# Attention and Fourier layer on one core: softmax weights transposed in 32x32 blocks and moved by transfers, order of work computed

## Chip, cores, metric

The kernel runs on one core of a Trainium2 chip. The metric is the device time of one execution in microseconds (us); smaller is better. The engines are called as in the profile: PE (TensorE), DVE (VectorE), ACT (ScalarE), POOL (GpSimd) and SP (SyncE, which here only issues transfers).

## What is computed

Two layers over x, 4096 rows (2 batches of 2048) of 512 float32 numbers. The reference, cut:

```python
x = x + xattn(layernorm(x), ctx, mask)      # 16 heads of 32, 128 keys a batch
x = x + ffn(layernorm(x))
# xattn: q = n @ wq + bq; k, v from ctx
# score = q k^T / sqrt(32) * mask; score == 0 -> -1e9
# context = softmax(score) v;  return context @ wo + bo
# ffn: real(ifft(fft(n) @ (w_re + i w_im))) + bias
```

Everything is float32. The second layer is linear in n, so the kernel builds one 512x512 matrix `m_ffn` from the Fourier weights once and then multiplies by it.

## The kernel before

The rows are cut into 32 tiles of 128, taken in eight groups `i` of four tiles `t`. In a tile:

- `scores` (L316): 16 small matmuls (32 deep, 128x128) fill two PSUM tiles `sc`, one for each half of eight heads.
- `Softmax` for each half (L335): DVE multiplies by the mask (`masked`, L345); turns zeros into the masked value and the sign round (L352) and takes the maxima (L354, scaled in L355); ACT takes eight exponentials with their sums (`exponentials`, L361); `divided` takes the reciprocal of the sums on DVE (L373) and multiplies the 128x1024 weights by it on POOL (L374).
- `transposed_weights` (L380): PE transposes the 16 heads' 128x128 weights (L400), ACT copies them to `pt` (L391).

Once per group:

- `Queries` (L285): four chains `q` of four matmuls, 512 columns wide. `query_statistics`, `query_norm` and `query_transposes` prepare their input: `relative` takes each row less its first element, bn_stats and aggregation on DVE (L219, L220), the deviation on POOL (L223, L224), normalization on DVE (L227), four transposes on PE (L194), a copy on ACT (L196).
- `context` (L414): 16 matmuls (L426) of `v` with the transposed weights, four copies on ACT (L434) to `cT`.

And for each tile, one or two groups later: `Project` (L446) is a chain `o`, added to the residual on DVE (L463), where POOL has added the bias (L442); the second normalization by the same steps (`ffn_statistics`, `ffn_norm`, `ffn_transposes`, with POOL adding the other bias, L482); `Ffn` (L489) is a chain `y`, added on DVE (L528), and a store from SP (L529). Every chain's matmuls are L210, in `chain`.

A float32 matmul shows as two MATMUL records and a float32 transpose as one. PSUM has two `sc` tiles of two banks and two banks each in `ps_tp` and `ps_mm`.

The order is written out by hand: each engine runs its instructions in the order in which the code gives them, and waits on semaphores. `slot` (L770) lays out one tile: scores, masks, then up to three chains, with the weight transposes of the tile before (`turned`) between them; lists such as `early`, `pool`, `on_a` or `end` place the other pieces. The first six and the last three tiles are written out piece by piece. Transfers go through SP: `load_rows` (L120), `load_residual` (L127), `load_mask` (L132) and the stores.

The Fourier preparation (`First`, `Second`, L659 and L732, with `half` and `m` tiles) and the keys and values run once, between the first tiles.

## Time and profile before

| | us |
|---|---|
| median of three timed runs | 526.06 (525.54 to 526.25) |
| span of the profiled execution, first to last instruction | 525.0 |
| timed median less that span | 1.06 |
| PE busy in the span | 517.2 |
| DVE busy | 443.9 |
| ACT busy | 343.3 |
| POOL busy | 336.4 |
| DMA: mean rate over the span | 69 GB/s |

The span comes from one profiled execution, the times from others without a profile. Busy is the union of an engine's instructions; a matmul's end is modelled, so a busy PE may still have room, and the start of one piece to the start of the next is the safer measure. The granted clock of PE is full in every slice. In a row of the groups of instructions stand line, engine, operation, the tiles written and read, the shape and count; then busy us and mean ns of one; then the idle time ahead of it and who ended it.

### The profile page before, as it was taken

The numbers are of one execution on the slowest core, as the hardware profiler recorded it, in microseconds if no ns is written. First come the engines' busy times: TensorE is split into PE (matmuls) and PEld (weight loads), VectorE is DVE, ScalarE is ACT, GpSimd is POOL, SyncE is SP. The second block draws the span as 40 slices with busy tenths as digits, with TensorE's granted clock in tenths as the row PEclk, the third lists the DMA queues.
The fourth block names the chain that finished last, engine by engine and source line by source line (L and its number), as shares of the span: only waits on it lengthen the run. The fifth ranks groups of instructions, "written<-read, shape, count | busy, mean of one in ns | idle before, by whom it ended". The sixth has DMA issues, their size and how long they took to land.

```text
span 525.0 us, 8834 instructions
## 1 busy us (share of the span) xinstructions
PE 517.2 (99%) x3028; PEld 293.0 (56%) x3028; DVE 443.9 (85%) x616; ACT 343.3 (65%) x1298; POOL 336.4 (64%) x286
## 2 busy tenths in 40 slices
PE   8999999999899999999999999999999999999997
PEld 7856685655445554555545555455545555555444
DVE  4889899999987999889997999989986899998351
ACT  3367799876666677766667777666686667666210
POOL 2769569996982579634993559634664466766450
PEclk9999999999999999999999999999999999999999
DMA  8962020000600042000600024000312001301002
GB/s 318 387 238 80 1 83 21 0 2 19 223 2 21 1 159 82 1 21 1 220 22 21 1 87 156 0 22 0 121 42 80 21 19 44 101 1 61 20 0 81
DMA packets 22892, 36.49 MB, mean 69 GB/s; under 512 B 2104, under 2 KB 7488, under 8 KB 22848
## 3 DMA queue, kind: packets, MB, share of 16 engines
q1 hardware_dynamic: 22160, 34.75, 19.1%
q10 hardware_dynamic: 688, 1.18, 0.6%
q8 instruction: 24, 0.39, 0.3%
q14 instruction: 20, 0.16, 0.1%
HBM read 27.53 MB, written 8.39 MB: 68 GB/s over the span
## 4 chain that ended last, share of the span: by engine, by line
PE 72%; DVE 17%; ACT 4%; POOL 4%; issue 2%; DMA 1%; SPq 0%; ACTq 0%; POOLq 0%; DVEq 0%
PE y L210 17%; PE o L210 16%; PE q L210 14%; PE tpw L400 7%; PE sc L326 5%; DVE w L352 4%; PE c L426 4%; ACT w L361 4%; DVE nmax L354 4%; DVE w L345 3%; PE tp_f L194 2%; PE tp_a L194 2%; PE k L570 1%; POOL w L374 1%; DVE nmax L355 1%
## 5 line engine op out<-in xcount | busy, mean ns | idle before, releaser
L361 ACT ACTIVATE w<-w,nmax 128x128 f32<-128x128 f32 x512 | 198.3, 394 | 22.4 <-DVE nmax L355 18.4
L374 POOL TENSOR_TENSOR w<-w,rden 128x1024 f32<-128x1024 f32 x62 | 120.4, 1947 | 65.1 <-DVE rden L373 54.7
L210 PE MATMUL o<-wo,cT 128*128 128x512 f32 x256 | 115.4, 594 | 0.0
L210 PE MATMUL y<-m_ffn,nT 128*128 128x512 f32 x248 | 112.5, 595 | 0.3 <-DVE nT L198 0.2
L210 PE MATMUL q<-xnT,wq 128*128 128x512 f32 (+1 forms) x256 | 111.8, 581 | 0.4 <-ACT cT L434 0.2
L391 ACT COPY pt<-tpw 128x512 f32<-128x512 f32 x120 | 64.1, 587 | 56.0 <-PE tpw L400 55.8
L361 ACT ACTIVATION_READ_ACCUMULATOR w<-w,nmax 128x1 f32 x512 | 98.8, 193 | 0.0
L352 DVE SCALAR_TENSOR_TENSOR w<-w 128x1024 f32<-128x1024 f32 x64 | 96.8, 1513 | 0.9
L345 DVE TENSOR_TENSOR w<-sc,mask 128x1024 f32<-128x1024 f32 x64 | 77.4, 1211 | 8.7 <-PE sc L326 8.2
L354 DVE TENSOR_REDUCE nmax<-w 128x8 f32<-128x1024 f32 x64 | 78.1, 1220 | 2.2
L400 PEld LDWEIGHTS tpw<-ident,w 128*128 128x128 f32 x496 | 57.5, 141 | 30.9 <-issue 28.1
L210 PEld LDWEIGHTS o<-wo,cT 128*128 128x128 f32 x256 | 46.2, 190 | 47.8 <-issue 46.2
L210 PEld LDWEIGHTS q<-xnT,wq 128*128 128x128 f32 x256 | 46.4, 190 | 46.1 <-issue 40.2
L210 PEld LDWEIGHTS y<-m_ffn,nT 128*128 128x128 f32 x248 | 44.5, 190 | 45.3 <-issue 43.5
L400 PE MATMUL tpw<-ident,w 128*128 128x128 f32 x496 | 65.0, 273 | 0.5 <-POOL w L374 0.4
L482 POOL TENSOR_TENSOR x<-x,bf 128x512 f32<-128x512 f32 x32 | 45.5, 1422 | 29.7 <-DVE norm_f L227 29.7
L223 POOL TENSOR_SCALAR rstd_f<-mv_f 128x1 f32<-128x1 f32 x32 | 19.0, 595 | 57.4 <-DVE mv_f L220 57.4
L442 POOL TENSOR_TENSOR x<-x,bo 128x512 f32<-128x512 f32 x32 | 45.5, 1450 | 0.0
L244 POOL TENSOR_SCALAR rel<-rows 128x512 f32<-128x512 f32 x24 | 42.7, 1792 | 0.5 <-PE k L570 0.5
L326 PEld LDWEIGHTS sc<-kT,qT 32*128 32x128 f32 x1024 | 31.5, 186 | 13.6 <-issue 11.4
L196 ACT COPY nT<-tp_f 128x512 f32<-128x512 f32 x29 | 16.8, 581 | 33.5 <-PE tp_f L194 33.4
L326 PE MATMUL sc<-kT,qT 32*128 32x128 f32 x1024 | 37.5, 283 | 0.0
(96 smaller groups left out, 532.6 us busy)
## 6 DMA issues: line engine op xcount, KB each, us to landing
rows<-in_x_dram SPq DMA_DIRECT2D x32, 256.0 KB, 4.6
x<-in_x_dram SPq DMA_DIRECT2D x32, 256.0 KB, 4.3
out_dram<-x SPq DMA_DIRECT2D x31, 256.0 KB, 2.0
mask<-in_mask_Bx1xSxS_fk_dram SPq DMA_DIRECT2D x8, 256.0 KB, 4.3
wk<-in_L_xattn_wk_w_dram ACTq DMA_DIRECT2D x2, 512.0 KB, 7.1
wq<-in_L_xattn_wq_w_dram SPq DMA_DIRECT2D x1, 1024.0 KB, 6.7
wr<-n_L_ffn_w_freq_real_dram SPq DMA_DIRECT2D x2, 512.0 KB
wi<-n_L_ffn_w_freq_imag_dram SPq DMA_DIRECT2D x2, 512.0 KB, 7.9
```

What stands on the lines that cost most here:

```text
L210: nc.tensor.matmul(ps, lhs(c), rhs(c), start=(c == 0), stop=(c == NC - 1))
L244: eng.tensor_scalar(d, xt, xt[:, 0:1], None, ALU.subtract)
L326: nc.tensor.matmul(sc[r // 2][:, r % 2, g, :], qTs[i][rows, g, t * P : (t + 1) * P], kT[rows, g, b * K : (b + 1) * K], start=True, stop=True,)
L345: nc.vector.tensor_tensor(self.w, self.sc.rearrange("p r g k -> p (r g) k"), self.mrow, ALU.mult)
L352: nc.vector.scalar_tensor_tensor(w, w, 0.0, w, ALU.is_equal, ALU.subtract)
L354: nc.vector.tensor_reduce(self.nmax, w, AX.X, ALU.min)
L361: nc.scalar.activation(w[:, h, :], w[:, h, :], AF.Exp, bias=self.nmax[:, h : h + 1], scale=-UNIT, accum_out=self.den[:, h : h + 1],)
L374: eng.tensor_tensor(w, w, rden.unsqueeze(2).to_broadcast([P, HH, K]), ALU.mult)
L391: nc.scalar.copy(dst, ps)
L400: nc.tensor.transpose(ps[:, r, :], ws[r // 2].w[:, (r % 2) * NC + g, :], ident)
L442: nc.gpsimd.tensor_tensor(xs[:, t, :], xs[:, t, :], bo, ALU.add)
L482: nc.gpsimd.tensor_tensor(xt, xt, bf, ALU.add)
```

## The change

The weights are no longer divided, and are no longer transposed on PE, except in the last tile.

- `blocks`: DVE transposes each half in 32x32 blocks (one instruction of 128x1024), into `Tw`. A block stays in its 32 partitions.
- `exchange`: 16 transfers a tile from SP move the blocks between the four sets of 32 partitions, each 32 rows of 2 KB (64 KB), from `Tw` to `pt`. A `pt` tile now holds the weights of two tiles.
- `Context`: the sums `den` of a whole group are inverted and transposed on DVE (`inverse`), written to HBM by eight small transfers (`collect`) and read back by four broadcasting ones of 256 KB (`spread`) into `rb`; `evict` multiplies the context by `rb` on DVE on its way out of PSUM. `pe` uses 32 matmuls of 256 columns, read in runs of 32.
- `Norm`: bn_stats works on the rows themselves (`relative` is gone); POOL forms deviation and `shift`, and ACT normalizes.
- `ps_tp` is merged into `ps_mm` (four banks); `w` has four buffers instead of five, `xnT` two instead of one.
- The written-out order and `slot` are gone. Behind the first tile's preparation every piece is entered with engine, cost, rank, needs and the buffers that it takes and gives; `emit` goes through them while the program is built and always takes the piece that its own clock lets start first (within `PATIENCE`, the lowest rank). That clock is arithmetic in the kernel's Python; on the chip the engines still only follow the resulting order and the semaphores. It treats POOL's pieces and DVE's `zeros` as excluding each other (`locks`).

The core of the diff:

```diff
-        def divided(self, eng=nc.gpsimd):
-            w = self.w
-            rden = small.tile([P, HH], FP, tag="rden", name=f"rden_{self.n}")
-            nc.vector.reciprocal(rden, self.den)
-            eng.tensor_tensor(
-                w, w, rden.unsqueeze(2).to_broadcast([P, HH, K]), ALU.mult
-            )
...
-    def transposed_weights(i, t, first, end, eng=None, banks=None, later=None):
-        if t == 0 and first == 0:
-            pts[i] = [big_tile("pt", 6, f"pt_{i}_{g}") for g in range(NC)]
-        ws = weights[i, t]
-        def copy(g, ps):
-            dst = pts[i][g][:, :, t * P : (t + 1) * P]
-            if eng:
-                eng.tensor_copy(dst, ps)
-            else:
-                nc.scalar.copy(dst, ps)
-        for g in range(first, end):
-            ps = (
-                banks[g]
-                if banks
-                else ps_tp.tile([P, NR, P], FP, tag="tp", name=f"tpw_{i}_{t}_{g}")
-            )
-            for r in range(NR):
-                nc.tensor.transpose(
-                    ps[:, r, :], ws[r // 2].w[:, (r % 2) * NC + g, :], ident
-                )
-            if later is not None:
-                later.append((copy, g, ps))
-            elif not banks:
-                copy(g, ps)
-        if banks and later is None:
-            for g in range(first, end):
-                copy(g, banks[g])
...
-    def context(i, first, end, eng=nc.scalar, spare=False):
-        b = place(i)[0]
-        if first == 0:
-            cTs[i] = big_tile("cT", 1, f"cT_{i}")
-        cT = cTs[i]
-        for g in range(first, end):
-            pool, tag = (ps_tp, "tp") if spare and 0 < g < NC - 1 else (ps_mm, "mm")
-            ps = pool.tile([P, GQ], FP, tag=tag, name=f"c_{i}_{g}")
-            for r in range(NR):
-                h = g * NR + r
-                nc.tensor.matmul(
-                    ps[r * DH : (r + 1) * DH, :],
-                    v[:, b, h * DH : (h + 1) * DH],
-                    pts[i][g][:, r, :],
-                    start=True,
-                    stop=True,
-                )
-            if eng is nc.scalar:
-                nc.scalar.copy(cT[:, g, :], ps)
-            else:
-                eng.tensor_copy(cT[:, g, :], ps)
...
+        def shift(self):
+            s = self.less = small.tile([P, 1], FP, tag="less", bufs=6, name=f"less_{self.name}")
+            nc.gpsimd.tensor_scalar(s, self.mv[:, 0:1], self.rstd, -1.0, ALU.mult, ALU.mult)
+        def norm(self, eng=None):
+            self.n = row_tile(self.tag, self.bufs, f"{self.tag}_{self.name}")
+            if eng is None or eng is nc.scalar:
+                nc.scalar.activation(
+                    self.n, self.src(), AF.Identity, bias=self.less, scale=self.rstd
+                )
...
+        def blocks(self, hf):
+            if hf == 0:
+                self.T = big.tile([P, NR, H, DH], FP, tag="Tw", bufs=2, name=f"Tw_{self.n}")
+            nc.vector.transpose(
+                self.T[:, :, hf * HH : (hf + 1) * HH, :],
+                self.w[hf].rearrange("p h (b j) -> p b h j", b=NR),
+            )
+        def exchange(self, b):
+            dst = weights_of(self.n)
+            for a in range(NR):
+                nc.sync.dma_start(
+                    dst[b * DH : (b + 1) * DH, a, :, :],
+                    self.T[a * DH : (a + 1) * DH, b, :, :],
+                )
...
+        def turn(self, hf, k):
+            ps = self.ps[hf, k] = bank(f"tpw_{self.n}_{hf}_{k}")
+            for r in range(NC):
+                nc.tensor.transpose(ps[:, r, :], self.w[hf][:, k * NC + r, :], ident)
+        def turned(self, hf, k, eng):
+            h = hf * HH + k * NC
+            copy(
+                eng,
+                weights_of(self.n)[:, :, h : h + NC, :].rearrange("p a h i -> p h a i"),
+                self.ps.pop((hf, k)).rearrange("p h (a i) -> p h a i", a=NR),
+            )
...
+    class Context:
+        def __init__(self, i):
+            self.i, self.ps = i, {}
+        def inverse(self):
+            den = dens.pop(self.i).rearrange("p t h -> p (t h)")
+            nc.vector.reciprocal(den, den)
+            self.rdT = small.tile([P, 2, DH], FP, tag="rdT", bufs=1, name=f"rdT_{self.i}")
+            nc.vector.transpose(self.rdT.rearrange("p k i -> p (k i)"), den)
+        def collect(self):
+            self.rd = dram.tile([H, GQ], FP, tag="rd", name=f"rd_{self.i}")
+            to = self.rd.rearrange("h (k t a i) -> a t h k i", k=2, t=2, a=NR)
+            for a in range(NR):
+                for t in range(2):
+                    p0 = a * DH + t * H
+                    nc.sync.dma_start(to[a, t], self.rdT[p0 : p0 + H])
+        def spread(self):
+            self.rb = big_tile("rb", 1, f"rb_{self.i}")
+            src = self.rd.rearrange("(r g) n -> r g n", g=NC)
+            for r in range(NR):
+                nc.sync.dma_start(
+                    self.rb[r * DH : (r + 1) * DH], src[r].partition_broadcast(DH)
+                )
+        def pe(self, g):
+            i = self.i
+            b = where(i * TG)[0]
+            ps = self.ps[g] = bank(f"c_{i}_{g}").rearrange("p a n -> p (a n)")
+            for u in range(2):
+                for r in range(NR):
+                    h = g * NR + r
+                    nc.tensor.matmul(
+                        ps[r * DH : (r + 1) * DH, u * 2 * P : (u + 1) * 2 * P],
+                        v[:, b, h * DH : (h + 1) * DH],
+                        pts[i * 2 + u][:, :, :, r * NC + g, :],
+                        start=True,
+                        stop=True,
+                    )
+        def evict(self, g):
+            i = self.i
+            if g == 0:
+                cTs[i] = big_tile("cT", 1, f"cT_{i}")
+            nc.vector.tensor_tensor(
+                cTs[i][:, g, :], self.ps.pop(g), self.rb[:, g, :], ALU.mult
+            )
...
+    LINK = 0.1
+    ROOM = {
+        "mm": 4, "sc": 2, "w": WBUFS, "Tw": 2, "norm": 2, "nf": 2, "nT": 2, "pt": 3,
+        "cT": 1, "xnT": 2, "qT": 2, "rows": 4, "x": 2, "mask": 2, "lane": 8, "rb": 1,
+    }
+    PATIENCE = {"PE": 0.3, "DVE": 0.2, "ACT": 0.15, "POOL": 0.2, "SP": 0.0}
...
+            for entry in waiting:
+                rank, k, p = entry
+                begin = max([q.end for q in p.needs], default=0.0)
+                for t in set(p.takes):
+                    n = p.takes.count(t)
+                    begin = max(begin, sorted(room[t])[n - 1] if len(room[t]) >= n else 1e9)
+                if begin >= 1e9:
+                    continue
+                for e, cost in p.engines:
+                    start = max(begin, free[e])
+                    if p.locks and e in held:
+                        start = max(start, held["POOL" if e == "DVE" else "DVE"])
+                    if e == "PE" and p.mode != mode:
+                        start = max(start, free[e] + 0.2)
+                    options.setdefault(e, []).append((start, rank, k, entry, cost))
+            best = None
+            for e, os in options.items():
+                first = min(o[0] for o in os)
+                o = min((o for o in os if o[0] <= first + PATIENCE[e]), key=lambda o: o[1:3])
+                if best is None or o[:3] < best[0]:
+                    best = o[:3], e, o
...
+            if p.kb:
+                arrived = max(arrived, start + 0.6) + p.kb / 280.0
+                p.end = max(free[e], arrived) + 1.4
+            else:
+                p.end = free[e] + LINK
...
+    def load(count, kb, rank, f, needs=(), takes=(), gives=()):
+        return piece(
+            [("SP", 0.43 * count)], rank, f, needs, list(takes) + ["lane"] * count,
+            list(gives) + ["lane"] * count, kb=kb * count,
+        )
+    SLOT = 13.6
...
+        for hf in range(2):
+            t0 = n * SLOT + hf * 5
+            p = dve(1.12, t0 + 1.3, lambda s=s, hf=hf: s.masked(hf), [sc, mask_in[i]], ["w"], ["sc"])
+            p = dve(1.12, t0 + 2.5, lambda s=s, hf=hf: s.zeros(hf), [p], locks=True)
+            p = dve(1.13, t0 + 3.6, lambda s=s, hf=hf: s.maxima(hf), [p], gives=["mask"] if t == TG - 1 and hf else [])
+            p = dve(0.09, t0 + 4.8, lambda s=s, hf=hf: s.units(hf), [p])
+            e1 = act(1.55, t0 + 5, lambda s=s, hf=hf: s.exponentials(hf, 0), [p])
+            e2 = act(1.55, t0 + 6.5, lambda s=s, hf=hf: s.exponentials(hf, 1), [e1])
+            exps.setdefault(i, []).append(e2)
...
+            if not last:
+                p = b_ = dve(1.13, t0 + 10.2, lambda s=s, hf=hf: s.blocks(hf), [p, b_], ["Tw"] if hf == 0 else [], ["w"])
...
+        if not last:
+            for b in range(NR):
+                p = load(
+                    4, 64, n * SLOT + 17, lambda s=s, b=b: s.exchange(b), [p],
+                    ["pt"] if n % 2 == 0 and b == 0 else [], ["Tw"] if b == NR - 1 else [],
+                )
...
+            need = sum((moved[i * TG + k] for k in range(TG)), [values_done])
+            d = dve(0.25, t0 - SLOT, c.inverse, exps[i])
+            d = load(8, 2, t0 - SLOT + 1, c.collect, [d])
+            d = load(4, 256, t0 - SLOT + 4, c.spread, [d], ["rb"])
```

## Prediction

> **What bounds the kernel now.** I read the page's first two parts, then the groups of instructions, then TensorE's timeline for one tile, then the waits of each engine, and last SyncE's timeline.
>
> ```profile
> span 525.0 us, 8834 instructions
> PE 517.2 (99%) x3028; PEld 293.0 (56%) x3028; DVE 443.9 (85%) x616; ACT 343.3 (65%) x1298; POOL 336.4 (64%) x286
> ```
>
> TensorE has 7.8 us without work. A busy PE need not be a needed PE, so I checked with one tile's timeline (start, duration):
>
> ```profile
> 115.58 1.17 PE L326 MATMUL sc<-kT,qT 32*128 32x128 f32 x32
> 116.68 1.09 PE L194 MATMUL tp_a<-ident,rel 128*128 128x128 f32 x8
> 117.61 3.60 PE L210 MATMUL o<-wo,cT 128*128 128x512 f32 x8
> 121.04 1.04 PE L400 MATMUL tpw<-ident,w 128*128 128x128 f32 x8
> 121.92 3.60 PE L210 MATMUL y<-m_ffn,nT 128*128 128x512 f32 x8
> 125.35 1.04 PE L400 MATMUL tpw<-ident,w 128*128 128x128 f32 x8
> 126.23 3.60 PE L210 MATMUL q<-xnT,wq 128*128 128x512 f32 x8
> 129.66 0.60 PE L194 MATMUL tp_f<-ident,norm_f 128*128 128x128 f32 x4
> ```
>
> Read starts, not durations: each piece begins before the modelled end of the one in front. A chain holds PE 3.43 us, scores 1.10, eight transposes 0.87, nothing idles. A tile's true demand is three chains 10.3, scores 1.1, weight transposes 1.75, two row transposes 0.95, a quarter of a context (3.58) 0.9: 15.0. SyncE's row loads for successive groups start at 190.17, 250.46 and 310.75, which is 60.3 per four tiles, 15.07 each. So PE sets the pace in every tile, and what is taken from PE counts in full until something else is late.
>
> The next in line is VectorE:
>
> ```profile
> L352 DVE SCALAR_TENSOR_TENSOR w<-w 128x1024 f32<-128x1024 f32 x64 | 96.8, 1513 | 0.9
> L345 DVE TENSOR_TENSOR w<-sc,mask 128x1024 f32<-128x1024 f32 x64 | 77.4, 1211 | 8.7 <-PE sc L326 8.2
> L354 DVE TENSOR_REDUCE nmax<-w 128x8 f32<-128x1024 f32 x64 | 78.1, 1220 | 2.2
> L374 POOL TENSOR_TENSOR w<-w,rden 128x1024 f32<-128x1024 f32 x62 | 120.4, 1947 | 65.1 <-DVE rden L373 54.7
> ```
>
> L352's median is 1225 ns and its longest 3190: the excess, 64 x 0.29 = 18 us, comes where it overlaps POOL, as at 255.25, where it took 2.49 beside L374 and L244.
>
> **The change, on TensorE.** It removes 16 transposes from each of 31 tiles (the last keeps them): 31 x 1.75 = 54 us. The context takes twice as many matmuls of half the columns, with its moving operand in runs of 32 elements. Bounds: nothing, to 128 further pairs of weight loads at 0.109 (28 us), if none lay behind matmuls. I take nothing: scores issue 32 loads in 1.10 us, and the strided loads of L677 took 196 ns against 190. PE alone would thus end at 525.0 - 54 = **471**.
>
> **On VectorE.** Removed: both normalizations (L227, 64 instructions, 59 us, to ACT), 64 reciprocals (0.11 from start to start), odd copies. Added: 62 block transposes, 32 context evictions with the inverse sums (0.64 each, as L463 and L528), eight small reciprocals and transposes. No row shows a VectorE transpose. Below, it costs 0.9 (two L227 of 512 elements, 0.45 apart when free); above, 2.44 (L354 twice). I take 1.17, L354's length less the 0.05 by which instructions overlap on average: it also reads one f32 input of 1024 elements.
>
> A page of the Trainium skill, "VectorE: DVE Perf Modes", section "Rules for kernel authors", speaks against the change: a 128x128 transpose belongs on TensorE. Its table "The three transpose paths" gives VectorE 311 ns for one 128x128 square; eight by themselves would be an estimated 2.49 us per half, 62 x 1.3 = 82 us above my sum, so about 575. I weigh it as one long instruction. No run here shows it yet.
>
> Per tile, from start to start (when free): mask 1.17, zeros 1.2, maxima 1.2, units 0.09, block transpose 1.17, all twice: 9.7. Three evictions at 0.64: 1.9. Two bn_stats with aggregation at 0.82: 1.6. Together **13.2**, against PE's 15.0 - 1.75 = 13.3. Contention stays where POOL reads beside `zeros`. POOL loses L374 and L244 (163 us) and keeps both bias additions (2 x 45.5) and two deviations a tile. Today's excess is 18 us on L352 and 10 on L355 (0.327 against 0.17). Bounds 0 and 28; I take 5, since the new order keeps `zeros` and POOL work apart, though only by its own clock.
>
> **The sum.** VectorE's first mask stays at 21.3. 32 x 13.2 = 422.4; contention 5; preparation after 21.3 (values 1.2; eight pairs L711 and L712, four at 1.48, four at 0.81) 10.4; less the last tile's block transposes, 2.4; less what VectorE does after the last softmax (context 2.6, projection and statistics 5.8, output 2.6, some two outputs still behind, 1.3) 12.3. The last maximum ends at 21.3 + 422.4 + 5 + 10.4 - 2.4 - 12.3 = 444.4.
>
> Then a chain that is now serial: eight exponentials 3.1, inverse 0.3, eight `collect` issues at 0.46 and one landing 2.0 (rows_m, the only SBUF to SBUF transfer in the trace), four `spread` issues 1.8 and a landing 4.3 (that of x), eviction 0.6: 15.8. Outputs of the group before run on PE meanwhile. From the first o of the last group to the end took 492.26 to 525.0, 32.7 now. 444.4 + 15.8 + 32.7 = **492.9**. Timed runs have a median of 526.06, 1.06 above this span: 494.
>
> **What I cost at nothing, and its cover.** ACT loses 31 x 4 copies at 0.5, gains two normalizations of 0.6 a tile; 16 exponentials 6.2 plus five other passes is 9 of 13.3. POOL has about 6 of 13.3. Uncovered, a copy delays a chain by its 0.6. A longer normalization (POOL's shift, 0.25) lies beside earlier outputs; without these, 0.25 each in the last group. SyncE gets 16 exchange transfers a tile, 2 collect, 1 spread, ahead of the loads and stores that wait in its order: 22.25 issues with row, residual, store and mask. Its pace:
>
> ```profile
> 190.17 1.82 SPq L120 DMA_DIRECT2D rows<-in_x_dram  x4
> 192.04 0.42 SPq L132 DMA_DIRECT2D mask<-in_mask_Bx1xSxS_fk_dram  x1
> 192.56 1.90 SPq L127 DMA_DIRECT2D x<-in_x_dram  x4
> 200.66 49.70 SPq L529 DMA_DIRECT2D out_dram<-x  x4
> ```
>
> Four issues in 1.82 to 1.90: 0.46 each, 10.2 a tile. The 49.70 is waiting for outputs: there is room. About 2.1 MB a tile in 13.4 us is 157 GB/s; the first 20 us moved 347. An exchange waits for the second block transpose, and loads and stores queue behind it. Rows are ranked nine tiles ahead of their use; a late store holds one residual buffer.
>
> Another page, "DMA: Bandwidth & Descriptors", sections "Bandwidth" and "Rules for kernel authors", advises against many small transfers and gives 0.95 us for 64 KB. Sixteen end to end would be an estimated 15.2 us a tile, above the pace, and the end, by the third rival's formula below, about 549 instead of 493. The x loads, issued 0.46 apart and landing after 4.3, already overlap here.
>
> **The rivals.**
>
> *TensorE stays the bound.* If a block transpose is 0.9 (62 x -0.27 = -17) and contention nil (-5), VectorE's path ends at 471, level with PE's 471, and 1 to 10 us of bubbles bring 472 to 482. For: L227 when free. Against: it has no reshaping to do. I give 0.20.
>
> *VectorE costs more.* At L374's 1.35 on VectorE, the transposes add 62 x 0.18 = 11; contention at half of its old 28 adds 9; an exchange landing at 4.3 instead of 2.0 adds some 2 for each of 8 contexts if PE has no other work, 16. Singly or together: 503 to 524, typically 510. For: the order is fixed by costs in the kernel that leave out POOL's lock on `units`. Against: neighbours of a stalled piece remain ready. 0.15.
>
> *SyncE's queue becomes the pace, and the kernel is slower.* In the loading stage four rows took 2.93 (start 8.88), 0.73 an issue. The last tile's scores are then at 21.3 + 31 p, its maximum some 8 later, its end 48.5 after that. This passes 525 when p is above 14.4, that is 0.65 an issue. At 0.73, p = 16.2: 580; at 0.67, p = 14.9: 540. For: 16 of these issues must run in order behind a wait. Against: at a quarter to a half of the DMA engines' load the rows show 0.46. That the exchange adds more work than it hides is this case too. 0.14.
>
> The forecast itself, VectorE and TensorE nearly level with VectorE late, covers 482 to 503 and has 0.50. Within 0.2% of the present time, about what a measurement can tell from no change, I leave 0.01, between the rivals. **So** faster 0.85, same 0.01, slower 0.14. The range 472 to 518 takes in the forecast, nearly all of the first rival and two thirds of the second.
>
> **What will show it.** The L400 group falls from 512 to 16; VectorE's busy share rises above 92% and PE's falls to 95% or so; row loads come about 54 us per group. The block transpose's mean: 1.2 supports the sum, above 1.7 it would be slower by that alone (32 us in 62). SyncE issue spacing tells the third rival. PE's waits by name show whether context waits for exchange landings. A granted clock below 1.0, through PE gaps, would void every PE price here.

## The result and the profile after

The changed kernel takes **577.07 us** (median of four runs, 575.61 to 577.9) beside 525.92 for the kernel before on the same chip: 1.097 times as long (95% interval 1.095 to 1.099). The forecast was 494, faster. The profiled execution has a span of 576.1 us, 83 more than the 492.9 of the sum. The head of the page, with TensorE's busy row and the granted clock by slices:

```profile
span 576.1 us, 8985 instructions
...
PE 492.4 (85%) x2788; PEld 259.6 (45%) x2788; DVE 446.3 (77%) x592; ACT 307.3 (53%) x1202; POOL 186.3 (32%) x298
...
PE   8869988557997999869997999899989984996797
...
PEclk9979998967999899989997999999999997899799
```

No engine is full any more. PE lost 25 us of busy time, not 54, because its pieces also stretched: where its row falls to 4, 5 or 6, the clock of that slice or the next falls to 6 to 8 tenths. Now three groups of instructions: two on VectorE, the new one and the one that contended with POOL, and the context on PE (busy us, mean ns, then idle time in front and who ended it):

```profile
L356 DVE STREAM_TRANSPOSE Tw<-w 128x1024 f32<-128x1024 f32 x62 | 76.2, 1233 | 32.9 <-DMA pt<-Tw 25.8
...
L327 DVE SCALAR_TENSOR_TENSOR w<-w 128x1024 f32<-128x1024 f32 x64 | 82.1, 1283 | 0.7
...
L421 PE MATMUL c<-pt,v 128*32 128x256 f32 x512 | 43.7, 500 | 35.4 <-DMA pt<-Tw 33.6
```

The disputed prices of VectorE came out as taken: a block transpose lasts 1.23 (1.17 was taken from start to start, the first began at 47.94 and the next instruction at 49.11), and `zeros` has a mean of 1283 instead of 1513, so contention, against the median of 1225 before, is 64 x 0.06 = 4 us. What is new stands at the end of the first and the last line: the block transposes wait 25.8 us for exchange transfers to free `Tw`, and PE waits 33.6 us in front of the contexts for exchanges to land. The contexts also stretched most: 43.7 us, against 29.4 (L426) in the kernel before. The chain that ended last, shares by engine, before; then the same and the shares by line, after:

```profile
PE 72%; DVE 17%; ACT 4%; POOL 4%; issue 2%; DMA 1%; SPq 0%; ACTq 0%; POOLq 0%; DVEq 0%
```

```profile
SPq 27%; PE 26%; DVE 20%; DMA 16%; ACT 4%; issue 4%; POOL 1%; DVEq 0%; ACTq 0%
SPq L365 19%; PE y L188 6%; PE o L188 6%; DMA rb<-rd 5%; SPq L403 5%; PE q L188 5%; DMA pt<-Tw 4%; DVE Tw L356 4%; DVE w L327 3%; DVE w L318 3%; DMA rd<-rdT 3%; DVE nmax L331 2%; ACT w L343 2%; PE c L421 2%; DMA x<-in_x_dram 2%
```

Before, SyncE's queue (SPq) held 0% of the chain. Now it is first, most of it `exchange`'s line L365. This is SyncE's timeline around the first group's context, and under it two of PE's pieces of the same time, with the wait in front of each in brackets:

```profile
97.52 16.80 SPq L365 DMA_DIRECT2D pt<-Tw  x24
114.42 0.53 SPq L111 DMA_DIRECT2D rows<-in_x_dram  x1
114.99 2.40 SPq L365 DMA_DIRECT2D pt<-Tw  x4
117.50 0.53 SPq L111 DMA_DIRECT2D rows<-in_x_dram  x1
118.07 5.60 SPq L403 DMA_DIRECT2D rd<-rdT  x8
124.93 1.73 SPq L410 DMA_DIRECT2D rb<-rd  x4
126.78 2.44 SPq L365 DMA_DIRECT2D pt<-Tw  x4
129.32 0.52 SPq L111 DMA_DIRECT2D rows<-in_x_dram  x1
129.89 19.91 SPq L365 DMA_DIRECT2D pt<-Tw  x28
```

```profile
119.17 5.63 PE L421 MATMUL c<-pt,v 128*32 128x256 f32 x56 [10.41 <-DMA pt<-Tw]
...
133.48 5.80 PE L188 MATMUL q<-xnT,wq 128*128 128x512 f32 x8 [6.96 <-DVE cT L433]
```

Read the queue from top to bottom: from 97.5 to 150 it issues with hardly a gap, and `collect`, whose eight transfers carry 4 KB each, stands behind 28 exchanges. PE waits 10.4 us at the context for the last exchange, then 7.0 because that context holds all four banks until `spread` has landed. Behind these waits eight matmuls of q last 5.80 instead of the 3.60 of other places, at the lowered clock. The four exchanges at 114.99 hold the queue until the next piece starts at 117.50, and eight collects take 5.0 in other groups: **0.63 us** an issue for both forms. `spread` takes 0.43, loads and stores about 0.5. A tile thus takes 16 x 0.63 + 2 x 0.63 + 0.43 + 0.53 (row) + 0.5 (residual) + 0.53 (store) + 0.14 (mask) = 13.5 us of issuing (the expectations below reckon with 14 to 14.1). Is the queue really full? From the last maximum of the fourth tile to the very last one, 422.7 us, all of SyncE's waits add up to 44 us. The longest:

```profile
SPq L410 <- DMA rd<-rdT: 9.5, 11, 2.2
SPq L365 <- DMA x<-in_x_dram: 8.7, 11, 1.3
SPq L365 <- DMA rb<-rd: 6.0, 11, 0.9
```

The other 379 us are issuing, with the short steps from one issue to the next: 54.1 for each of seven groups, which is 4 x 13.5. SyncE is full there for 90% of the time.

**Three marks** make runs comparable: the start of the last maximum (`tensor_reduce`) of the fourth tile, the mean time from one group's last maximum to the next, and the time from the very last maximum to the end. In the forecast a group is 4 x 13.2 + 5/8 of contention = 53.4, the last maximum starts at 443.2 (444.4 is its end), so the fourth tile's at 443.2 - 7 x 53.4 = 69.4.

| | span | tile 4's last maximum | a group | last maximum | from there to the end |
|---|---|---|---|---|---|
| before | 525.0 | 72.1 | 58.3 | 480.4 | 44.6 |
| forecast | 492.9 | 69.4 | 53.4 | 443.2 | 49.7 |
| after | 576.1 | 90.8 | 60.4 | 513.5 | 62.6 |

The 83 us split into 21 at the start, 7 x 7.0 = 49 in the groups, and 13 at the end.

### The profile page after: what moved, and what is told of

The parts are those of the page before. It is cut to its first block, busy times and chain, and to the rows that moved or that the text cites. A ratio compares the mean times of both kernels' runs of the same rounds, so it can differ in the third digit from the quotient of the medians.

```text
span 576.1 us, 8985 instructions
## 1 busy us (share of the span) xinstructions
PE 492.4 (85%) x2788; PEld 259.6 (45%) x2788; DVE 446.3 (77%) x592; ACT 307.3 (53%) x1202; POOL 186.3 (32%) x298
## 4 chain that ended last, share of the span: by engine, by line
SPq 27%; PE 26%; DVE 20%; DMA 16%; ACT 4%; issue 4%; POOL 1%; DVEq 0%; ACTq 0%
SPq L365 19%; PE y L188 6%; PE o L188 6%; DMA rb<-rd 5%; SPq L403 5%; PE q L188 5%; DMA pt<-Tw 4%; DVE Tw L356 4%; DVE w L327 3%; DVE w L318 3%; DMA rd<-rdT 3%; DVE nmax L331 2%; ACT w L343 2%; PE c L421 2%; DMA x<-in_x_dram 2%
## 5 line engine op out<-in xcount | busy, mean ns | idle before, releaser
L188 PE MATMUL q<-xnT,wq 128*128 128x512 f32 (+2 forms) x288 | 119.3, 560 | 10.1 <-DVE cT L433 7.0
L188 PE MATMUL y<-m_ffn,nT 128*128 128x512 f32 x248 | 116.2, 613 | 0.7 <-ACT nT L195 0.7
L356 DVE STREAM_TRANSPOSE Tw<-w 128x1024 f32<-128x1024 f32 x62 | 76.2, 1233 | 32.9 <-DMA pt<-Tw 25.8
L327 DVE SCALAR_TENSOR_TENSOR w<-w 128x1024 f32<-128x1024 f32 x64 | 82.1, 1283 | 0.7
L188 PEld LDWEIGHTS q<-xnT,wq 128*128 128x128 f32 x288 | 52.3, 196 | 63.5 <-issue 47.9
L217 POOL TENSOR_SCALAR rstd_f<-mv_f 128x1 f32<-128x1 f32 x32 | 8.1, 253 | 216.8 <-DVE mv_f L213 122.7
L421 PE MATMUL c<-pt,v 128*32 128x256 f32 x512 | 43.7, 500 | 35.4 <-DMA pt<-Tw 33.6
L472 POOL TENSOR_TENSOR x<-x,bf 128x512 f32<-128x512 f32 x32 | 42.4, 1326 | 20.7 <-ACT nf_f L227 20.5
L421 PEld LDWEIGHTS c<-pt,v 128*32 128x32 f32 x512 | 20.5, 141 | 59.5 <-issue 45.3
L238 PE MATMUL tp_f<-ident,nf_f 128*128 128x128 f32 x128 | 20.6, 285 | 19.1 <-ACT nf_f L227 11.7
L482 DVE TENSOR_TENSOR x<-y,x 128x512 f32<-128x512 f32 x31 | 21.1, 680 | 16.6 <-PE y L188 16.3
```

What stands on the lines that cost most here:

```text
L188: nc.tensor.matmul(ps, lhs(c), rhs(c), start=(c == 0), stop=(c == NC - 1))
L327: nc.vector.scalar_tensor_tensor(w, w, 0.0, w, ALU.is_equal, ALU.subtract)
L356: nc.vector.transpose(self.T[:, :, hf * HH : (hf + 1) * HH, :], self.w[hf].rearrange("p h (b j) -> p b h j", b=NR),)
L421: nc.tensor.matmul(ps[r * DH : (r + 1) * DH, u * 2 * P : (u + 1) * 2 * P], v[:, b, h * DH : (h + 1) * DH], pts[i * 2 + u][:, :, :, r * NC ...
L472: eng.tensor_tensor(xt, xt, bf, ALU.add)
```

## Experiments

My theory was that SyncE's queue, by the number of its issues, is the new bound. The rivals: bytes moved or partitions crossed; a wrong order (the clock of `emit` uses other prices and starting times); TensorE's or VectorE's own work. Each run's expectation names its own theories A and B. The marks of the runs (times are medians; the interval is that of the ratio to the kernel before):

| run | us | ratio, interval | tile 4 | a group | to the end |
|---|---|---|---|---|---|
| e1_one_issue | 546.9 | 1.039 (1.035 to 1.044) | 89.6 | 56.3 | 62.4 |
| e2_start | 568.4 | 1.080 (1.077 to 1.083) | 82.2 | 60.1 | 64.0 |
| e3_hbm | 580.8 | 1.104 (1.101 to 1.107) | 90.4 | 60.7 | 63.9 |
| e4_pe | 581.1 | 1.104 (1.096 to 1.113) | 88.6 | 60.7 | 64.0 |
| e5_both | 536.8 | 1.021 (1.018 to 1.023) | 80.2 | 56.3 | 62.3 |
| e7_tail | 567.8 | 1.081 (1.076 to 1.085) | 81.5 | 61.3 | 56.0 |
| e8_mixed | 571.7 | 1.087 (1.083 to 1.091) | 80.2 | 60.7 | 63.8 |
| e9_prices | 592.1 | 1.126 (1.124 to 1.128) | 78.4 | 64.2 | 62.4 |
| e10_banks | 584.8 | 1.110 (1.106 to 1.114) | 82.6 | 60.1 | 81.5 |
| e11_actq | 569.4 | 1.082 (1.079 to 1.085) | 78.1 | 60.7 | 62.2 |
| e12_one | 521.5 | 0.991 (0.989 to 0.993) | 81.1 | 54.4 | 56.7 |
| e13_straight | 582.2 | 1.109 (1.106 to 1.112) | 81.7 | 59.3 | 82.0 |
| e14_fours | 523.3 | 0.995 (0.993 to 0.996) | 81.4 | 54.9 | 56.0 |
| e15_pool4 | 533.6 | 1.014 (1.011 to 1.017) | 78.0 | 55.9 | 62.0 |
| e16_loads | 561.0 | 1.067 (1.064 to 1.071) | 79.4 | 60.1 | 57.5 |
| e17_split | 531.0 | 1.010 (1.008 to 1.011) | 77.9 | 55.8 | 60.7 |
| e18_pool8 | 549.0 | 1.044 (1.042 to 1.046) | 79.7 | 57.2 | 68.6 |
| e19_three | 553.6 | 1.052 (1.050 to 1.054) | 79.2 | 55.9 | 80.4 |

One caution governs the reading. A piece's price or needs go into `emit`, so most edits change the order of everything behind them; so does the slot (`SLOT`, the time per tile by which `emit` ranks the pieces). Only these pairs share one computed order: after and e1, after and e2, e2 and e5, e10 and e13, e12 and e14, e15 and e17. Their differences are clean; between other runs the order is part of the difference.

### Few issues, and an earlier start

e1_one_issue:

```diff
-            for a in range(NR):
-                nc.sync.dma_start(
-                    dst[b * DH : (b + 1) * DH, a, :, :],
-                    self.T[a * DH : (a + 1) * DH, b, :, :],
-                )
+            if b == 0:
+                nc.sync.dma_start(dst, self.T)
```

> One transfer of 1 MB a tile copies the transposed blocks to where they are, instead of 16 transfers of 64 KB that exchange them between the sets of 32 partitions: the same bytes, the same order of all other work, 15 issues fewer on SyncE in each of 31 tiles. The exchange itself is left out. Theory A (SyncE's queue sets the pace: 16 issues at 0.63 us and six others make 14 us a tile): groups follow each other after 54 us instead of 57.6, the stretch from 97 to 118 us in which SyncE issues without a break shrinks by some 15, and the time falls to 525 to 540. Theory B (the loss is made in the start, by PE and DVE pieces that wait in order, and by the order's wrong clock; SyncE is only late with them): at most 10 us better, 566 to 576.

Measured 546.9: 30.2 less, from the groups (56.3 instead of 60.4, 7 x 4.1 = 29). The waits of PE for `pt` are gone from its list. The time is above the 525 to 540 that I gave SyncE's queue, and the gain is three times what the rival allowed. The edit changes three things at once, the number of transfers, their size and the crossing of partitions; e13 and e15 below take them apart.

e2_start:

```diff
-    for t in range(TG, 2 * TG):
-        load_rows(t)
...
             nc.sync.dma_start(to[:, cs, :], parted(of[rs, :]))
+    for t in range(TG, 2 * TG):
+        load_rows(t)
     nc.sync.dma_start(wv, chunks(wv_w))
```

> The loads of the Fourier weights wr and wi are issued ahead of the second four row tiles, which wait for their buffers anyway; nothing else changes. Theory B: POOL's wait of 8.3 us for wr goes, the query normalizations behind it, the values on PE and the first block transposes on DVE come some 10 us earlier, and the time falls by 10 to 15, to 561 to 566, with groups still 57.6 apart. Theory A alone (SyncE is busy without a break from 97 us on and absorbs an earlier start): 571 to 577.

The reason for it stands in the changed kernel's first 50 us, in three engines' timelines: SyncE, POOL and VectorE.

```profile
10.28 7.43 SPq L111 DMA_DIRECT2D rows<-in_x_dram  x4
17.76 1.28 SPq L160 DMA_DIRECT2D wr<-n_L_ffn_w_freq_real_dram  x2
```

```profile
25.12 2.34 POOL L591 TENSOR_TENSOR cols<-wr 128x1020 f32<-128x1020 f32 x1 [8.34 <-DMA wr<-n_L_ffn_w_freq_real_dram]
```

```profile
47.27 0.69 DVE L582 TENSOR_TENSOR v<-v,bv 128x512 f32<-128x512 f32 x1 [13.96 <-PE v L188]
```

For comparison, SyncE in the kernel before, and the changed kernel's wait at the second four row loads:

```profile
8.88 2.93 SPq L120 DMA_DIRECT2D rows<-in_x_dram  x4
11.87 0.90 SPq L164 DMA_DIRECT2D wr<-n_L_ffn_w_freq_real_dram  x2
```

```profile
SPq L111 <- DVE norm_a L231: 8.0, 4, 2.2
```

These four loads now take 7.43 instead of 2.93: each waits for a normalization (L231), which reads the rows themselves and so holds their buffer. wr and wi are issued behind them, 6 us later than before; POOL's `add_columns` waits; behind it in POOL's order are the deviations of tiles 4 to 7; ScalarE's normalizations, PE's transposes and the values follow; VectorE stands still for 14.0 with work queued behind `v`. With wr and wi first, 568.4: 8.7 less, tile 4 at 82.2 instead of 90.8. That lies between the two forecasts; the groups stay as they were (60.1 against 60.4; the 57.6 of the two expectations was too low a reading of the pace). e5_both puts both edits together:

> Loads of wr and wi ahead of the row loads of tiles 4 to 7, and one transfer of 1 MB per tile (partition to partition, no exchange between partitions, so its output isn't the reference's) in place of 16. Alone the first gave 568.4 against 577.1 (-8.7), the second 546.9 (-30.2). Theory A (SyncE's queue sets the pace and the late start is a sum of its own): the two add, 538, between 534 and 542. Theory B (a queue that is late absorbs a late start, the same wait seen twice): less than the sum, 543 to 547.

Measured 536.8, 31.6 below e2 and 10.1 below e1: the two add. They are two causes, and all other runs but e3 and e4 have the earlier start.

### Is it bytes, or TensorE's own work?

e3_hbm sends the blocks through HBM: one store of 1 MB, then four loads of 256 KB a tile.

```diff
+            nc.sync.dma_start(self.xd, self.T.rearrange("p b h j -> p b (h j)"))
...
+            src = self.xd.rearrange("(a p) b n -> b p a n", a=NR)
+            nc.sync.dma_start(dst, src[b])
```

> The exchange goes through HBM: one store of 1 MB and four loads of 256 KB a tile, 5 issues instead of 16, the result complete; the order is computed anew with these pieces. Theory A: SyncE needs 5 x 0.45 + 6.25 x 0.5, about 6 us a tile, PE or DVE set the pace at 13.4 to 13.8, groups 54 us apart, time 520 to 540. Theory B: the start stays, at most 10 us better, 566 to 576. A third one, C (bytes, not issues: 3.1 MB a tile through 16 DMA engines that were already half busy): 570 or more, with context waiting for landings.

580.8, no better: theory A missed, and the time is in C's range. SyncE's issues are few here, but its waits show another queue: each set of loads waits in order for its store.

```profile
SPq L370 <- DMA xd<-Tw: 83.5, 20, 8.0
```

Five issues with a wait in the middle came out no cheaper than sixteen without. PE waits here too for landings at the context (14.6 us for the loads), so this run alone doesn't exclude bytes; e1 and e5, which move as many bytes as the change in few issues, do.

e4_pe undoes the block transposes alone: every tile goes the last tile's way over TensorE, with inverse sums, ScalarE's normalizations and a computed order kept.

```diff
+    PE_TILES = lambda n: True
...
             last = n == NT - 1
-            if not last:
+            pes = last or PE_TILES(n)
+            if not pes:
```

> Block transposes and exchange are undone: all tiles take the last tile's path, 16 transposes on PE and four copies on ACT or DVE. Inverse sums on the context, normalization on ACT and the computed order stay. Theory A: SyncE issues 6.25 transfers a tile and is out of the way, PE needs 15.1 us a tile as in the kernel before, 60.3 a group; with the slower start the time is 530 to 545, better than the whole change although PE does more. Theory B (start and order): 560 or more.

581.1, with no exchange at all: theory A missed here too. PE is 96% busy from 200 to 300, and a group is 60.7: TensorE's old bound, 4 x 15.0, is back (the kernel before has 58.3 by this mark), with the late start (88.6) and the longer end (64.0) on top. So the new form costs 36 us at the start and the end against the kernel before (16.5 + 19.4), and 17 in the groups (7 x 2.4), even where SyncE is free. The full queue is not its only loss.

e8_mixed does this for odd tiles only, with the earlier start, measured prices and a slot of 14.2 in place of e4's 13.6; against e4:

```diff
-    PE_TILES = lambda n: True
+    PE_TILES = lambda n: n % 2
```

> Nothing left out. With wr and wi loaded first and the measured prices in the order; odd tiles are transposed by TensorE (8 transposes and their copies, as the last tile), even tiles by VectorE and the exchange, slot 14.2. SyncE's issues fall from 14.1 to about 9 us a tile, TensorE's demand rises from 13.3 to 14.2 and VectorE's falls by half a tile's block transposes. Theory A (SyncE's issues are the pace): 535 to 550. Theory B (the computed order and engines that wait for one another are): 558 or more, as the run with all tiles on TensorE (581) suggests.

571.7 with groups of 60.7: no gain from half the issues. Theory A missed. PE is 94 to 96% busy from 200 to 400 and waits 20.5 us for a context's banks in front of transposes. Which of the two keeps it at 60.7 isn't separated; TensorE's added work is too near to the pace for this run to test SyncE.

### Is it the order's clock, and the banks?

e9_prices has the same instructions as e2, in an order computed with measured prices:

```diff
-            [("SP", 0.43 * count)], rank, f, needs, list(takes) + ["lane"] * count,
+            [("SP", (price or 0.5) * count)], rank, f, needs, list(takes) + ["lane"] * count,
...
-    SLOT = 13.6
+    SLOT = 14.6
...
-    emit({"PE": 16.0, "DVE": 16.5, "ACT": 17.0, "POOL": 20.0, "SP": 5.0}, 30.0)
+    emit({"PE": 20.2, "DVE": 19.0, "ACT": 20.7, "POOL": 22.1, "SP": 22.3}, 33.0)
```

> Nothing left out. wr and wi loaded first, and the order computed anew with the prices and starting times of the trace (exchange and collect 0.63 us an issue, other loads 0.5, normalization 0.73, VectorE's passes 1.17 to 1.2, engines free at 19 to 22 us, slot 14.6). Same instructions as the start run (568.4). From one group's last maximum to the next it took 60.1 us there. Theory A (SyncE's issues, 14.1 us a tile, are the pace whatever the order): 560 to 570, groups 59 to 60. Theory B (the order followed a wrong clock, and engines in fixed order wait for one another): below 556, groups 57 or less.

592.1: slower by 24, and outside both ranges. The theory of a wrong clock falls, at least in this form. (The same prices with a slot of 14.2, e6_prices, give an order in which the engines wait for one another without end, so it has no time.) One wait holds more than that difference: first SyncE's timeline, then PE's.

```profile
432.79 10.24 SPq L364 DMA_DIRECT2D pt<-Tw  x16
443.08 5.03 SPq L402 DMA_DIRECT2D rd<-rdT  x8
449.51 1.73 SPq L409 DMA_DIRECT2D rb<-rd  x4
```

```profile
457.71 5.87 PE L187 MATMUL q<-xnT,wq 128*128 128x512 f32 x8 [33.68 <-DVE cT L432]
```

A context was placed before its sums were spread; it held the four banks for 33.7 us while `collect` stood behind sixteen exchanges. e10_banks makes the context need the spread, with a slot of 14.4 instead of 14.6:

```diff
-                    0.86, t0 + g / 10, lambda c=c, g=g: c.pe(g), need + [p], ["mm"] + (["cT"] if g == 0 else []),
+                    0.86, t0 + g / 10, lambda c=c, g=g: c.pe(g), need + [p, d], ["mm"] + (["cT"] if g == 0 else []),
```

> Nothing left out. As the run with new prices (slot 14.4), and the context's matmuls are placed only when the spread inverse sums should have landed, so that the context doesn't hold all four banks while it waits for them. Theory A (each group's outputs wait behind banks held for the spread, 7 us and a lowered clock after it): 8 to 14 us below the run with new prices, most of it after the last maximum, where 64 us become 52 to 56. Theory B (the chain of the inverse sums is hidden but for the last group, and there it only moves in front of the context): within 3 us of it.

584.8, 7.3 less than e9, but not where theory A put it: groups fell from 64.2 to 60.1, and the end grew from 62.4 to 81.5, because the projections of four more tiles were still to do there (64 against 32 matmul records of o, eight a tile). Inconclusive as a price of the banks; the waits of up to 33.7 are gone.

e7_tail takes the chain of sums out of the last group alone, and divides its weights on VectorE:

```diff
+            if i == NG - 1:
+                p = dve(1.3, t0 + 9.8, lambda s=s, hf=hf: s.divide(hf), [p])
...
-            d = load(8, 2, t0 - SLOT + 1, c.collect, [d])
+            d = None if whole else load(8, 2, t0 - SLOT + 1, c.collect, [d])
```

> Nothing left out. With wr and wi loaded first; in the last group alone the weights are divided on VectorE before they are transposed (8 passes of 1.2 us more), the context is copied without the inverse sums, and its collect and spread are gone. Against 568.4. Theory A (the serial chain inverse, collect, spread, eviction is a sum of its own at the end, some 12 to 16 us, of which the added passes give back up to 9): 555 to 562. Theory B (the end waits for outputs on TensorE, the chain is hidden beside them): 566 to 575.

567.8 against 568.4. From the last maximum to the end it is 8.0 less (56.0 against 64.0), but that maximum comes 7.6 later (510.3 against 502.7). Theory A's 12 to 16 were 8 at most, for one projection fewer is left for the end (32 matmul records of o against 40), and the added passes gave all of it back. The total is in B's range, though not for B's reason alone.

### The number of issues

e12_one is e10 with one straight transfer a tile, as in e1; `emit` reckons 4 x 0.16 us of SyncE for each quarter of the exchange.

> One transfer of 1 MB per tile, partition to partition, in place of the 16: the exchange between partitions is left out. Otherwise as the run with banks, its order computed with that one issue. It shows what the change would be worth if its exchange were free to issue. With the old order and wr, wi first this was 536.8, groups of 56.4. Theory A (what is left above the forecast is the order: TensorE and VectorE wait for one another, and the context holds the banks): 515 to 527. Theory B (VectorE's own work, 53.9 a group, with an unavoidable start and end, is the rest): 530 to 538.

**521.5**, 63 us below e10 and 0.9% below the kernel before, with the exchange left out. SyncE's longest waits, first in e10, then in e12:

```profile
SPq L485 <- DVE x L481: 45.6, 9, 24.1
SPq L364 <- DVE Tw L355: 27.5, 6, 9.6
```

```profile
SPq L364 <- DVE Tw L355: 119.9, 25, 11.0
SPq L482 <- DVE x L478: 69.7, 12, 20.3
```

In e10 SyncE came late to most block transposes, so it seldom waited for one; in e12 it waits 119.9 us for them: it has room. And PE and DVE are 96.8 and 97.1% busy from 200 to 300, level, as the forecast had them. Which part of "one straight transfer" does it? e13_straight keeps e10's order and its sixteen transfers, but without crossing:

```diff
-                    dst[b * DH : (b + 1) * DH, a, :, :],
+                    dst[a * DH : (a + 1) * DH, b, :, :],
```

> As the run with banks (584.8), with its order and its 16 transfers of 64 KB a tile, but each goes to the partitions that it came from: the exchange between partitions is left out. Theory A (the number of issues is the cost): 578 to 590. Theory B (crossing partitions is the cost, in the transfer or in its issue): near the run with one straight transfer, 521 to 540.

582.2 against 584.8: crossing partitions costs nothing that shows. What is left is the number, or that the sixteen consist of runs of 2 KB and the one of 8 KB; e15 below, which has the same runs in three queues, speaks for the number. e14_fours has e12's order and four transfers of 256 KB a tile:

```diff
+            nc.sync.dma_start(
+                dst[b * DH : (b + 1) * DH], self.T[b * DH : (b + 1) * DH]
+            )
```

> As the run with one straight transfer of 1 MB a tile (521.5), in four transfers of 256 KB instead: SyncE's issues take some 6.6 us a tile instead of 4.7; the exchange between partitions is left out. Theory A (issues cost nothing while SyncE has slack, and become the pace near 14 us a tile): 519 to 526. Theory B (every issue costs its 0.63 us of delay to the weights, so 3 more are a fifth of the way from 521.5 to 584.8): 531 to 537.

523.3 against 521.5: three more issues a tile are nearly free while the queue has room. What costs is not 0.63 for each issue, it is the full queue.

### A complete kernel with the issues shared

e11_actq moves 4 of the 16 to ScalarE's queue; e16_loads moves the loads of rows, residuals and masks there too; e15_pool4 instead moves 4 more to GpSimd's:

```diff
+            eng = (nc.sync, nc.sync, nc.gpsimd, nc.scalar)[b]
             for a in range(NR):
-                nc.sync.dma_start(
+                eng.dma_start(
```

> Nothing left out. As the run with banks, and 4 of the 16 exchange transfers of a tile are issued from ScalarE's queue: SyncE's issues fall from 14.1 to 11.6 us a tile, ScalarE gains 2.5. Theory A (SyncE's issues are the pace): groups of 57 or less instead of 60, that is 15 to 25 us below the run with banks. Theory B (issues that wait for a block transpose hold up ScalarE's exponentials, which come in fixed order behind them): no gain, or slower by up to 20.

> Nothing left out. As the run with 4 exchange transfers of a tile on ScalarE's queue (569.4; slot 14.2), and the loads of rows, residuals and masks, 2.25 a tile, are issued by ScalarE too, so that exchanges don't stand behind loads that wait for a buffer: SyncE's issues fall from 11.6 to about 10.5 us a tile, ScalarE's rise by 1.1. Theory A (SyncE's issues and the waits in its order are the pace): 545 to 562. Theory B (ScalarE becomes the queue that holds up others): 570 or more.

> Nothing left out. As the run with 4 exchange transfers of a tile on ScalarE's queue (569.4), and 4 more on GpSimd's: SyncE keeps 8, its issues fall from 11.6 to 9.1 us a tile. Theory A (SyncE's issues are the pace): 535 to 555. Theory B (GpSimd's way of issuing is dearer, and its deviations, in fixed order behind it, hold up the normalizations): 570 or more.

569.4, 561.0 and **533.6**. e11's total is in theory A's range, but its groups are 60.7, not 57; what it gained is e10's long end, so it doesn't show A. Its queue isn't full either: in the groups SyncE waits 119 us, against 60 in e10, and the longest row is one that e10 doesn't have, for landings of other exchanges:

```profile
SPq L365 <- DMA pt<-Tw: 37.3, 16, 9.7
```

So what SyncE was relieved of came back as waits; whose landings hold it up isn't settled. e16 (slot 14.2 where e11 and e15 have 14.4) has groups of 60.1 and likewise no shown gain in pace. With SyncE down to eight exchanges a tile, e15 has 55.9: 36 us less than e11, 51 less than e10 (in other orders). GpSimd's issues cost 0.52 each:

```profile
L365 POOL DMA_DIRECT2D pt<-Tw x124 | 63.5, 518 | 23.1 <-DVE Tw L355 19.7 <-issue 2.3 <-DMA rd<-rdT 0.5
```

A page of the Trainium skill, "DMA: Bandwidth & Descriptors", section "Issuing engines are not separate DMA queues", says that starting transfers from several engines saves only the sequencer's time for starting them, usually small beside the transfer. What is saved here is that time, as the page says; but 13.5 us of it a tile were not small beside a pace of 13.4, and the landing of 2.0 us each overlapped.

The last three add to e15. e17_split lets ScalarE issue half of `collect` and `spread` in the last group; e18_pool8 gives GpSimd eight of the sixteen and ScalarE none; e19_three leaves SyncE four, GpSimd eight, ScalarE four.

```diff
-                    nc.sync.dma_start(to[a, t], self.rdT[p0 : p0 + H])
+                    eng = nc.scalar if t and self.i == NG - 1 else nc.sync
+                    eng.dma_start(to[a, t], self.rdT[p0 : p0 + H])
```

> Nothing left out. As the run with 4 exchange transfers on ScalarE's and 4 on GpSimd's queue (533.6), and in the last group half of collect and spread is issued by ScalarE, which has nothing to do then. Theory A (the chain of the inverse sums is bare at the end, and its 12 issues in a row are part of it): 6 of 12 issues of 0.43 to 0.63 us go, 3 us less, 529 to 532. Theory B (landings, not issues, set the chain): 533 to 535.

> Nothing left out. As the split run, but 8 exchange transfers of a tile go to GpSimd's queue and none to ScalarE's; SyncE keeps 8. An issue on GpSimd took 0.52 us there. Theory A (SyncE's issues were the pace, and ScalarE's four stood in its normalizations' and exponentials' way): 522 to 529. Theory B (GpSimd's issues, some 4 us a tile in blocks of 2, hold up its deviations, and with them the normalizations): 533 or more.

> Nothing left out. As the split run, with 4 exchange transfers of a tile on SyncE, 8 on GpSimd and 4 on ScalarE: SyncE's issues fall from 9.1 to 6.6 us a tile. Theory A (issues cost only when their queue is full, as the run with four straight transfers suggests, and SyncE has slack at 9.1 already): within 4 us of the split run, 526 to 534. Theory B (each issue that SyncE loses is still worth time): 522 or less.

531.0, 549.0 and 553.6. The split brings 2.7, as theory A of it said, at the edge of what the two intervals tell apart. e18 is where its theory B had it; e19 misses both ranges: e19's last maximum, at 470.7, comes as early as e17's 468.7, and what it loses is 20 us of outputs left for the end (64 records of o against 32). So SyncE's further relief is worth nothing in pace, and GpSimd's eight issues or the new order cost the rest; these two aren't separated. The best complete kernel of this study, 531.0, stays 1.0% above the kernel before.

## Why the prediction was wrong

- **The step that failed first**: "Four issues in 1.82 to 1.90: 0.46 each, 10.2 a tile", costed at nothing because "there is room". I took the price of row and residual loads for the exchange and for `collect`. Both issue at 0.63: 13.5 a tile, above the 13.4 of VectorE with its contention. A dearer issue stood in the profile before, in the one transfer from SBUF to SBUF whose landing of 2.0 I used:

  ```profile
  74.50 3.16 SPq L721 DMA_DIRECT2D rows_m<-half  x4
  ```

  Its four issues last 592 ns in the median, as the exchange's do (588). What makes an issue dear isn't shown: `collect` goes to HBM and costs as much, the 1 MB copy of e1 from all 128 partitions lasts 513 ns, and e3's 1 MB store from them 338. On one order this is 30 to 32 us (e1 against after, e5 against e2); with an order computed for few issues, e12 against e10, up to 63, of which the order is a part. The pace in groups fell from 60 to 54.4.
- **The rival named it, and its formula did not.** "SyncE's queue becomes the pace" had 0.14, and 0.63 lay just under its threshold of 0.65. It reckoned the pace as issues alone; by it 13.5 a tile would end at 496. The trace shows issues plus waits in order, the exchange behind loads and broadcasts, `spread` behind the landing of `collect`: 60.4 a group, of which 54 are issues and 6 waits. It also left the start and the end as they were.
- **The start**: "VectorE's first mask stays at 21.3" (it was 3 us off: 24.4, and the first maximum starts at 28.6 instead of 25.8), and the rest of the first group was taken to follow. Without `relative` the normalization reads the rows themselves, so their buffers come free later, and three queues pass that on. 21 us; moving the loads of wr and wi gets 9 to 10 of it back. I had looked at added instructions, not at what now releases a row buffer.
- **The end**: "Outputs of the group before run on PE meanwhile." Not while a context holds four banks. Behind the last context PE's next piece waits for the evictions, which wait for `spread`:

  ```profile
  524.26 3.66 PE L421 MATMUL c<-pt,v 128*32 128x256 f32 x64
  535.23 1.09 PE L238 MATMUL tp_f<-ident,nf_f 128*128 128x128 f32 x4 [7.31 <-DVE cT L433]
  ```

  The windows from the last maximum's end to the end of the span, before and after (length, then busy time of PE first; the clock is the third figure from the right):

  ```profile
  481.60:525.00 43.40, 40.00 (x148) 19.39 (x146) 17.25 (x31) 9.05 (x26) 16.04 (x17) 0.99 0.12 43
  ```

  ```profile
  514.70:576.10 61.40, 49.43 (x196) 24.53 (x194) 19.38 (x35) 8.47 (x25) 13.79 (x21) 0.92 0.21 61
  ```

  PE is busy 9 us longer there, and 12 instead of 3 without work: 13 above the sum.
- **Right**: VectorE's own demand. 446.3 us busy, as the sum implies; block transpose 1.17 from start to start, contention 4 against 5, exchange landing 2.0 as taken. On PE, twice as many matmuls in the context were rightly taken as free: 30.1 us in e12 against 29.4 before. With the queue out of the way (e12) the kernel ran at 54.4 a group against 53.4, 25.9 us above the sum in all: 12 at the start, 7 in the groups, 7 at the end. The clock was named as what would void PE's prices, and did. One sum is off: the three terms of "VectorE costs more" add 36, so together they end at 530, not 524.
- **The two pages weighed**: by "VectorE: DVE Perf Modes", "The three transpose paths", a half's transposes were an estimated 2.49 us (the page's figure is for bfloat16, the weights are float32); the trace shows 1.23, and the measurement decides. By "DMA: Bandwidth & Descriptors", "Rules for kernel authors", many small transfers are to be avoided. Its direction held, for another reason than the transfers' own length: the same bytes without crossing took 582.2 in sixteen transfers and 523.3 in four (in another order), while each of the sixteen landed 2.0 us after its issue, beside the others.

What stays open: how much of e12's gain over e10 is the order's, what holds the start 12 us above the sum even in e12, why half or three quarters of the exchanges on SyncE (e8, e11) brought no better pace than all of them, and why computed orders with truer prices ended worse.

## What to carry to other kernels

Price a DMA issue by the row of its own form, or of the nearest form in the trace, and add up the issuing queue like an engine, with the waits that stand in it; as long as it has room its issues are free, and when it is full everything queued behind it is late. Where an engine takes over an operation, ask which buffer is now released later and which loads stand behind that one. Where an order is computed, compare only kernels with the same order, or read the pace of the groups and the work left at the end apart from each other.

## What the runs showed of the hardware

- An issue on SyncE took 0.63 us for transfers between partitions of SBUF (64 KB) and for `collect` (4 KB, SBUF to HBM in many short runs), about 0.5 for loads and stores of 256 KB, 0.43 for the broadcasts of 256 KB. Bytes don't set it in these rows: e14's transfers between SBUF of 256 KB issue at 0.63 as well. On GpSimd the same exchange took 0.52 an issue.
- VectorE's transpose in 32x32 blocks, 128x1024 in one instruction, takes 1.23 us, the same as a pass that reads one input of that size.
- ScalarE's normalization with bias and scale per partition, 128x512, takes 0.81 us beside 0.58 for a copy (the prediction had 0.6).
- Behind waits of TensorE the granted clock is lower. Contexts that last 3.66 at the full clock take 4.5 to 6.1 behind waits of 2.6 to 10.4 us (the clock was 0.53 in 186.4 to 192.7), and a chain of 3.60 took 5.80 behind a wait of 7.0 (0.63 in 133.4 to 139.3).
